# Shared experts in pieces of two products, projections and output in parts, and seven shared blocks behind the routed experts

## The chip, the cores and the metric

One Trainium2 chip, one of its cores. The metric is the time of one execution on the device in microseconds; the median of several executions counts. A profile of one execution comes with it. PE is TensorE, DVE is VectorE, ACT is ScalarE, POOL is GpSimd, SP is SyncE, which only issues DMAs.

## The reference

One transformer layer of fp32 over `x` of shape (4, 1024, 256): `x + attention(xn) + ffn(xn)`, with `xn = layernorm(x)` for both branches.

```python
qkv = (xn @ W_qkv + b_qkv)                       # 16 heads of 16, rotary on q and k
attn = softmax(q @ k.T / sqrt(16))               # 1024 x 1024 per head and batch
attention = (attn @ v) @ W_out + b_out

scores = sigmoid(xn @ w_gate.T)                  # 16 experts, 4 groups of 4
w, idx = grouped_top4(scores)                    # 2 best groups, 4 best experts, weights normed
routed = sum over 4 experts of w * swiglu(xn, w1_e, w3_e, w2_e)     # hidden size 128
shared = silu(xn @ w1_s.T) * (xn @ w3_s.T) @ w2_s.T                 # hidden size 256
ffn = routed + shared
```

## The kernel before

Everything runs in one stream of 256 **steps** of attention, into which all other work is mixed by hand. A group is one batch (b, 0 to 3) and four heads (g, 0 to 3); each of the 16 groups has 16 steps, s = 0 to 15. `Attention.step` makes one step:

- Two **quartets** of matmuls. Each of the four matmuls of a quartet uses 32 rows of TensorE and fills one PSUM bank of 128x512. Two are scores for the exponentials of this group (`ps`, L1225, evacuated by ScalarE as `es`, L1234), two are scores for the row maxima of the next group (`pm`, L1183, reduced by VectorE, L1191). The last 16 steps have no next group, and there all eight matmuls are of the first kind.
- Between the quartets (`between`) the **units** of this step: all other work of TensorE.
- After them the product of the step's exponentials with the values (`av`, L1250), one step late. `av_part(2)` makes it whole behind the second quartet. If the next step has no units (`more` is false), `av_part(0)` makes only the first half there, and the next step makes the second half between its quartets.

TensorE takes its instructions strictly in this order (`k.pe`), and so does SP (`k.sp`). All PSUM tiles come from one pool of eight banks (`k.bank`); the bank of each is fixed when the program is built. One bank holds `av` for eight steps.

`pieces(step)` gathers the units of a step. `Attention.own` gives what the attention needs itself: `max_off` (the maxima into q, steps s = 2 and 10), `normalise` (s = 3 and 11), for the batches 1 to 3 projections and their transposes (`project_unit` every other step for 16 steps, `turn_unit` three steps after each), and per half batch the output projection, `finish`, as a turn and in the next step a product of 8 matmuls and two adds to `acc`. Then come the others:

- **Shared experts.** 16 blocks of 256 rows, of three units each (`shared_block`): two of `first(c)`, one for each half of the hidden size, with gate and up products in one bank (`hidden`: tanh on ScalarE, two operations on VectorE), and `last`, the output product of two times two matmuls in one bank and one add of 128x512 to the rows of x (`xb`, loaded by SP, with the bias added by POOL). The block is stored to `acc` in DRAM in the next step. From step 10 three units come in seven steps, up to 36 units (12 blocks); the other four blocks come after the routed experts, two units in five steps (steps 173 to 200). These units come whether or not the step has other work.
- **Routed experts.** Routing on VectorE and POOL from step 9; from step 33 two rows of slots per step are written by indirect DMA (`put`); from step 98 one pair of tiles per step (`expert_units`), 72 pairs and a last output, with their weights loaded by SP two steps ahead; from step 171 two gathers per step (`get`, POOL) and two sums (`add`, L1011, VectorE), onto rows of `acc` that SP loads first.

`acc` of the half batches is fetched by SP (`fetch_acc`) before `finish` adds to it. `reload` brings the transposed input of batches 2 and 3 back from DRAM (1 MB); the first unit of a batch's first shared block calls for the next batch's (`want`), at steps 38 and 66.

A step without units is called **empty** below.

Of the kernel before, what the change touches and what calls it, by code (L numbers as in the profile page):

```python
# [8 lines left out]
F32 = mybir.dt.float32  # L9
I32 = mybir.dt.int32  # L10
AF = mybir.ActivationFunctionType
# [4 lines left out]
P = 128  # L16
# [26 lines left out]
SHARED = ((10, 36),)  # L43
# [6 lines left out]
def kernel(  # L50
# [166 lines left out]
    n_put = NT * TOPK  # L217
    done = {"shared": 0}
    tiles, ex = None, None

    def pieces(step):

        nonlocal tiles
        now = norm.pieces(step, att.own(step))
        while routing_tensor:
            now.append(routing_tensor.pop(0))
        due = 0
        if SHARED[0][0] <= step:
            due = min(SHARED[0][1], 1 + (step - SHARED[0][0]) * 3 // 7)
        if tiles is not None and not tiles:  # L230
            due = min(len(shared), SHARED[0][1] + (step - TILES_FROM - PAIRS) * 2 // 5)
        while done["shared"] < due:
            now.append(shared[done["shared"]])
            done["shared"] += 1
        if step == TILES_FROM:
            tiles = beside.expert_units(ex.enter_context(ex_pool()))
        if tiles:
            now.append(tiles.pop(0))
            if not tiles:
                done["tiles"] = step  # L240
        return now
# [41 lines left out]
class Kit:  # L283


    def __init__(self, tc, banks):
        self.tc, self.nc, self.banks = tc, tc.nc, banks
        self.last_sp = self.last_exp = None
        self.ranking = self.slots_known = False
        self.summed = 0  # L290
# [490 lines left out]
class Beside:  # L781
# [51 lines left out]
    def shared_block(self, blk):  # L833
        k, nc = self.k, self.nc
        b, at = divmod(blk * SL, T)
        st = {"gu": []}

        def first(c):
            def run():
                if c == 0:  # L840
                    st["x"] = self.ff.tile([P, R, C], F32, name=f"xb_{blk}", tag="y", bufs=3)
                    k.sp(st["x"], k.rows(k.xf, blk * R, R))
                    nc.gpsimd.tensor_tensor(
                        st["x"], st["x"], k.bo_sb.unsqueeze(1).to_broadcast([P, R, C]), ALU.add
                    )
                if at == 0 and c == 0:
                    self.want(b)
                fs = slice(c * P, (c + 1) * P)
                st["gu"].append(
                    self.hidden(  # L850
                        self.xnT[b][:, :, at : at + SL],
                        [(k.w1s_sb[:, :, fs], k.w3s_sb[:, :, fs])], f"s{blk}_{c}",
                    )
                )
            return run

        def last():
            po = k.bank([P, R, C], f"pso_{blk}")
            for r in range(R):
                for c in range(FS // P):  # L860
                    k.pe(
                        nc.tensor.matmul(  # L862
                            po[:, r, :],
                            lhsT=st["gu"][c][:, r * P : (r + 1) * P],
                            rhs=k.w2s_sb[:, c, :],
                            start=(c == 0), stop=(c == FS // P - 1),
                        )
                    )
            nc.vector.scalar_tensor_tensor(st["x"], po, 0.5, st["x"], ALU.mult, ALU.add)
            self.later.append(lambda: k.sp(k.rows(k.acc, blk * R, R), st["x"]))  # L870

        return [first(0), first(1), last]

    def want(self, b):

        for n in range(1, B):
            if n not in self.back and n <= b + 1:
                self.reload(n)
# [105 lines left out]
    def get(self):  # L984
# [5 lines left out]
        if kk == 0:  # L990
            self.yg = self.rows.tile([P, TOPK, C], F32, name=f"yg_{t}", tag="yg", bufs=3)
# [33 lines left out]
class Attention:  # L1025
# [7 lines left out]
    def __init__(self, ctx, k, wqkv_sb, bqk_sb, bv_sb, wout_sb, cos_sb, sin_sb):  # L1033
# [26 lines left out]
        self.av, self.accs, self.stores = {}, {}, []  # L1060
# [4 lines left out]
    def project_unit(self, b, t):  # L1065
        self.product(b, t)
        self.rotate(b, t)

    def product(self, b, t):
        nc, k = self.nc, self.k  # L1070
        if t == 0:
# [10 lines left out]
        n0 = t * P  # L1082
        ps = [k.bank([P, HALF], f"pqk_{b}_{t}"), k.bank([P, C + E], f"pv_{b}_{t}")]

        for half, w in ((0, HALF), (1, C if b else C + E)):
            for c in range(NC_):
                k.pe(
                    nc.tensor.matmul(  # L1088
                        ps[half][:, :w],
                        lhsT=self.xnT[b][:, c, n0 : n0 + P],  # L1090
                        rhs=self.wqkv_sb[:, c, half * HALF : half * HALF + w],
                        start=(c == 0),
                        stop=(c == NC_ - 1),
                    )
                )
# [8 lines left out]
        else:  # L1104
# [5 lines left out]
            qk.rearrange("p h d -> p (h d)"), ps[0], self.bqk_sb, ALU.add  # L1110
        ).ins

        nc.scalar.copy(
            self.vv[b][:, t, : H * VS].rearrange("p (h d) -> p h d", d=VS)[:, :, :DH],
            ps[1][:, :C].rearrange("p (h d) -> p h d", d=DH),
        )
        if b == 0:
            nc.scalar.copy(self.logits[:, t, :], ps[1][:, C:])
        self.qk = qk, rot
# [167 lines left out]
    def fetch_acc(self, b, qh):  # L1287
        k = self.k
        t1 = b * TT + qh * 4 + 4
        assert b + 1 < B or k.summed >= t1  # L1290
# [6 lines left out]
    def finish(self, b, qh):  # L1297
# [15 lines left out]
        def product():  # L1313
            acc = self.accs[b, qh]
            for pr in range(2):
                py = k.bank([P, 2, C], f"py_{b}_{qh}_{pr}")
                for i in range(2):
                    for c in range(NC_):
                        k.pe(
                            nc.tensor.matmul(  # L1320
                                py[:, i, :],
                                lhsT=oc[:, c, 2 * pr + i, :],
                                rhs=self.wout_sb[:, c, :],
                                start=(c == 0),
                                stop=(c == NC_ - 1),
                            )
                        )
                part = acc[:, 2 * pr : 2 * pr + 2, :]
                nc.vector.tensor_tensor(part, part, py, ALU.add)
            to = k.outf if b == B - 1 else k.acc  # L1330
            self.stores.append(lambda: k.sp(k.rows(to, b * TT + qh * 4, 4), acc))

        return turn, product
# [11 lines left out]
    def own(self, at):  # L1345
# [16 lines left out]
        if self.projects(at):  # L1362
            out.append(lambda: self.project_unit(*self.projects(at)))
        if self.projects(at - 3):
            out.append(lambda: self.turn_unit(*self.projects(at - 3)))
        if g == 0 and b > 0 and s == 5:
            self.parts = self.finish(b - 1, 1)
            out.append(self.parts[0])
        last = 13 if b + 1 < B else 14
        if g == NG - 1 and s == last:  # L1370
            self.parts = self.finish(b, 0)
            out.append(self.parts[0])
        if g == 0 and b > 0 and s == 6 or g == NG - 1 and s == last + 1:
            out.append(self.parts[1])
        return out

    def step(self, units, more, bits):
# [48 lines left out]
        if g == NG - 1:  # L1426
            if s == (7 if b + 1 < B else 12):
                self.fetch_acc(b, 0)
            if s == 15 and b + 1 < B:
                self.fetch_acc(b, 1)  # L1430

    def last_steps(self):
# [8 lines left out]
        for turn_or_product in self.finish(b, 1):  # L1441
            turn_or_product()
# [59 lines left out]
```

## Time and profile before

| | |
|---|---|
| median of 3 executions | 1421.13 us (1420.94 to 1421.87) |
| profiled execution | 1426.41 us, its span 1424.7 us |
| granted TensorE clock, mean | 0.995 |
| PE, DVE, ACT, POOL busy | 98%, 65%, 55%, 30% of the span |
| DMA | 199 MB, 140 GB/s |
| matmul records | 9878, two for each fp32 matmul |

The span is the time from the first to the last instruction; the profiled execution's time has 1.7 us more around it. The steps are not marked in the trace; step n begins with the es number 4n of ScalarE, here taken from its timeline:

| steps | what lies beside the attention | us |
|---|---|---|
| 9 to 97 | routing, shared experts, puts, projections of batches 1 and 2 | 443.6 |
| 98 to 170 | routed experts, projections of batches 2 and 3 | 524.3 |
| 171 to 203 | gathers, shared experts | 152.0 |
| 204 to 239 | gathers | 131.9 |
| 240 to 255 and the end | last group, output | 53.1 |

A busy time is the union of an engine's instructions, with the ends of matmuls modelled; a row of the timeline has start and length in us; a row of groups has its count, then its busy time in us and the mean length of one in ns, then idle time before it.

### The profile page before, as it was taken

Reading aid. Unit: us, or ns where it says so; the run is one execution under the profiler, and the core shown is the slowest. Engines: PE = TensorE matmul, PEld = TensorE weight load, DVE = VectorE, ACT = ScalarE, POOL = GpSimd, SP = SyncE. Lnnn points to the kernel's source line nnn. Section 1 sums busy time; section 2 is a strip of 40 time slices with the busy share of each in tenths; the row PEclk is TensorE's granted clock in tenths of the full one; section 3 lists DMA queues with packets and bytes.
Section 4 is the critical chain, followed back from the end, with each engine's and each line's share of the span. In section 5 each row is a group of like instructions: output and inputs, shape, how many; then the busy total and the mean of one; then the engine's idle time right before and its main releaser. Section 6 shows DMA issues by size and latency. Waiting matters only on the chain.

```text
span 1424.7 us, 26637 instructions
## 1 busy us (share of the span) xinstructions
PE 1400.7 (98%) x9878; PEld 683.9 (48%) x9878; DVE 925.4 (65%) x1702; ACT 780.8 (55%) x1586; POOL 423.0 (30%) x498
## 2 busy tenths in 40 slices
PE   7899999999999999999999999999999999999998
PEld 4443344443444344566566665656564344433333
DVE  6878867668766675444555555554445888899941
ACT  4565544455544555555555555554555555566575
POOL 5401503664443445220000000001224444455500
PEclk9899999999999999999999999999999999999999
DMA  5134743523242224446666666665551334333310
GB/s 185 62 124 167 256 169 115 174 75 104 91 139 92 90 78 141 148 149 189 209 209 201 203 197 216 190 208 168 169 152 56 109 119 130 112 108 111 104 39 30
DMA packets 136673, 199.15 MB, mean 140 GB/s; under 512 B 13920, under 2 KB 99040, under 8 KB 136288
## 3 DMA queue, kind: packets, MB, share of 16 engines
q1 hardware_dynamic: 103088, 137.78, 30.7%
q0 software_dynamic: 12288, 33.57, 7.6%
q10 hardware_dynamic: 21168, 26.10, 5.2%
q8 instruction: 78, 1.28, 0.4%
q14 instruction: 51, 0.42, 0.1%
HBM read 124.01 MB, written 79.69 MB: 143 GB/s over the span
## 4 chain that ended last, share of the span: by engine, by line
PE 97%; DVE 1%; ACT 1%; DMA 0%; issue 0%; POOL 0%; ACTq 0%; DVEq 0%
PE pm L1183 22%; PE ps L1225 19%; PE av L1250 19%; PE ph_r L813 9%; PE exy L947 5%; PE ph_s L813 4%; PE pqk L1088 4%; PE ext L938 2%; PE pso L862 2%; PE py L1320 2%; PE ptr L1164 2%; PE pv L1088 2%; PE po L1274 1%; PE pmt L1206 1%; DVE mx L1191 1%; PE pt L472 1%
## 5 line engine op out<-in xcount | busy, mean ns | idle before, releaser
L1234 ACT ACTIVATE es<-ps 128x512 f32<-128x512 f32 x1024 | 554.8, 596 | 412.6 <-PE ps L1225 228.1
L1191 DVE TENSOR_REDUCE mx<-pm 128x1 f32<-128x512 f32 x1024 | 659.5, 683 | 167.0 <-PE pm L1183 103.4
L1183 PE MATMUL pm<-kT,qT 32*128 32x512 f32 x1792 | 523.1, 641 | 1.4 <-ACT kT L1169 1.4
L1225 PE MATMUL ps<-q,kT 32*128 32x512 f32 x1792 | 506.2, 640 | 0.9 <-DVE q L1211 0.8
L1250 PE MATMUL av<-es,vv 128*32 128x512 f32 (+1 forms) x2576 | 287.4, 517 | 0.0
L1225 PEld LDWEIGHTS ps<-q,kT 32*128 32x128 f32 x1792 | 143.3, 183 | 168.0 <-ACT es L1234 85.1
L1183 PEld LDWEIGHTS pm<-kT,qT 32*128 32x128 f32 x1792 | 157.7, 183 | 66.2 <-issue 23.3
L1250 PEld LDWEIGHTS av<-es,vv 128*32 128x32 f32 x2576 | 51.5, 108 | 240.5 <-issue 216.4
L903 POOL DMA_INDIRECT xs<-rows,slot_i x128 | 123.7, 967 | 128.3 <-DVE mx L1191 111.5
L994 POOL DMA_INDIRECT yg<-ys,slot_i x128 | 121.8, 952 | 126.5 <-DVE mx L1191 121.0
L821 DVE SCALAR_TENSOR_TENSOR th_r<-th_r,ph_r 128x256 f32<-128x256 f32 x72 | 30.3, 421 | 195.9 <-ACT th_r L820 195.9
L1128 POOL TENSOR_TENSOR rot<-qk,sin_sb 128x256 f32<-128x256 f32 x56 | 39.5, 726 | 372.5 <-DVE qk L1109 372.0
L813 PE MATMUL ph_r<-xT,w 128*128 128x128 f32 x1152 | 140.5, 275 | 0.5 <-ACT xT L941 0.5
L813 PEld LDWEIGHTS ph_r<-xT,w 128*128 128x128 f32 x1152 | 134.4, 192 | 0.8 <-ACT xT L941 0.7
L1183 PE MATMUL pm<-qkT,qkT 32*128 32x512 f32 x256 | 78.5, 640 | 1.3 <-DVE mx L1191 1.3
L947 PE MATMUL exy<-w,gu_r 128*128 128x256 f32 x288 | 77.3, 391 | 0.0
L1225 PE MATMUL ps<-q,qkT 32*128 32x512 f32 x256 | 75.4, 640 | 0.3 <-DVE gu_s L823 0.3
L820 ACT ACTIVATE th_r<-ph_r 128x256 f32<-128x256 f32 x72 | 27.7, 384 | 81.1 <-PE ph_r L813 81.1
L947 PEld LDWEIGHTS exy<-w,gu_r 128*128 128x128 f32 x288 | 50.0, 190 | 28.7 <-issue 19.7
L1011 DVE SCALAR_TENSOR_TENSOR sum<-yg,wk,sum 128x256 f32<-128x256 f32 x128 | 60.7, 474 | 0.0
L953 ACT ACTIVATE y<-exy 128x512 f32<-128x512 f32 x72 | 43.8, 608 | 17.7 <-PE exy L947 17.4
L1080 POOL MEMSET vv<- 128x128 f32 x4 | 1.3, 318 | 143.6 <-ACT es L1234 143.6
(178 smaller groups left out, 1224.7 us busy)
## 6 DMA issues: line engine op xcount, KB each, us to landing
w<-we SPq DMA_DIRECT2D x144, 384.0 KB
xs<-zero ACTq DMA_DIRECT2D x8, 2304.0 KB
xg<-xs SPq DMA_DIRECT2D x72, 256.0 KB
ys<-y SPq DMA_DIRECT2D x72, 256.0 KB
acc<-acc SPq DMA_DIRECT2D x14, 512.0 KB
xb<-in_x_dram SPq DMA_DIRECT2D x16, 256.0 KB
acc<-xb SPq DMA_DIRECT2D x16, 256.0 KB
we<-in_w_dram ACTq DMA_DIRECT2D x4, 1024.0 KB
```

The source lines that it names most:

```text
L813: nc.tensor.matmul(ph[:, n, at], lhsT=w[n][:, c, :], rhs=xT[:, c, at], start=(c == 0), stop=(c == NC_ - 1),)
L903: put = nc.gpsimd.indirect_dma_start(out=k.xs, out_offset=bass.IndirectOffsetOnAxis(ap=k.slot_i[:, t, kk : kk + 1], axis=0), in_=self.rows ...
L947: nc.tensor.matmul(py[:, r, :], lhsT=gus[i][:, r * P : (r + 1) * P], rhs=got[i][1][:, r, 2 * NC_ * F :], start=True, stop=True,)
L953: nc.scalar.activation(y, py, AF.Copy, scale=0.5)
L994: get = nc.gpsimd.indirect_dma_start(out=self.yg[:, kk, :], out_offset=None, in_=k.ys, in_offset=bass.IndirectOffsetOnAxis(ap=k.slot_i[:, ...
L1011: nc.vector.scalar_tensor_tensor(sm[:, 0, :], yg[:, kk, :], k.wk[:, t, kk : kk + 1], sm[:, 0, :], ALU.mult, ALU.add)
L1088: nc.tensor.matmul(ps[half][:, :w], lhsT=self.xnT[b][:, c, n0 : n0 + P], rhs=self.wqkv_sb[:, c, half * HALF : half * HALF + w], start=(c = ...
L1183: nc.tensor.matmul(ps, lhsT=self.qT[b, g // 2][rows, g % 2, qt * P : (qt + 1) * P], rhs=self.kT[b, g // 2][rows, g % 2, hf * HALF : (hf + ...
L1191: k.pace = nc.vector.tensor_reduce(out=self.mx_of[b, g, qt // 4][hf][:, qt % 4, j, :], in_=ps, axis=AX.X, op=ALU.max,).ins
L1225: nc.tensor.matmul(ps, lhsT=self.kT[b, g // 2][rows, g % 2, kc * P : (kc + 1) * P], rhs=self.q2[b, g, qh][rows, :], start=True, stop=True,)
L1234: k.last_exp = nc.scalar.activation(e, ps, AF.Exp, scale=DH**-0.5).ins
L1250: nc.tensor.matmul(av[32 * j : 32 * j + 32, cols], lhsT=self.vv[b][:, kc, h * VS : h * VS + 32], rhs=es[j][:, cols], start=(kc == 0), stop ...
```

## The change

Shared blocks are cut finer: `gate(c)` and `up(c)` are one product each (4 matmul records of 128x256, a bank of their own), `last(r)` is the output product of 128 rows with an add of 128x256: six **half pieces** a block, 96 in all. Nine blocks (54 pieces) come before step 98, seven (42 pieces) after the routed experts. A piece is given to a step that has no units; to one that has, only when the count is behind a line. `project_unit` becomes the product for q and k with the rotation, and in the next step that for the values; the product of `finish` is four products, one in each of four steps, with an add of 128x256 each. The transposed input of batch 3 is reloaded at step 110, `fetch_acc` of a second half batch comes at s = 3 of the next group instead of s = 15. `shared_rows` only serves the assertions that `acc` is stored before it is read.

```diff
-SHARED = ((10, 36),)
+SHARED_FROM = 10
+SHARED_FIRST = 9
+RELOAD_AT = 110
...
+    k.at_step[RELOAD_AT] = lambda: beside.reload(B - 1)
...
-        due = 0
-        if SHARED[0][0] <= step:
-            due = min(SHARED[0][1], 1 + (step - SHARED[0][0]) * 3 // 7)
-        if tiles is not None and not tiles:
-            due = min(len(shared), SHARED[0][1] + (step - TILES_FROM - PAIRS) * 2 // 5)
-        while done["shared"] < due:
-            now.append(shared[done["shared"]])
+        n, first = done["shared"], SHARED_FIRST * len(shared) // (NT * P // SL)
+        if tiles is None and SHARED_FROM <= step < TILES_FROM and n < first:
+            left = TILES_FROM - 1 - step
+            late = n < first - left * (first + 6) // (TILES_FROM - SHARED_FROM)
+        elif tiles is not None and not tiles and n < len(shared):
+            m, since = n - first, step - TILES_FROM - PAIRS
+            late = m < since * 4 // 5 if since <= 25 else m < 18 + (since - 25) * 24 // 34 - 4
+        else:
+            late = None
+        if late or late is not None and not now:
+            now.append(shared[n])
             done["shared"] += 1
...
+        def half(c, n):
+            ph = k.bank([P, SL], f"ph_s{blk}_{c}_{n}")
+            w = (k.w1s_sb, k.w3s_sb)[n]
+            for i in range(NC_):
+                k.pe(
+                    nc.tensor.matmul(
+                        ph, lhsT=w[:, i, c * P : (c + 1) * P],
+                        rhs=self.xnT[b][:, i, at : at + SL],
+                        start=(i == 0), stop=(i == NC_ - 1),
+                    )
+                )
+            return ph
...
-        def first(c):
+        def gate(c):
...
+                ph = half(c, 0)
+                th = st["th"] = self.ff.tile([P, SL], F32, name=f"th_s{blk}_{c}", tag="th")
+                nc.scalar.activation(th, ph, AF.Tanh, scale=0.5)
+                nc.vector.scalar_tensor_tensor(th, th, 1.0, ph, ALU.add, ALU.mult)
             return run
+        def up(c):
+            def run():
+                ph = half(c, 1)
+                gu = self.ff.tile([P, SL], F32, name=f"gu_s{blk}_{c}", tag="gu", bufs=3)
+                nc.vector.tensor_tensor(gu, st["th"], ph, ALU.mult)
+                st["gu"].append(gu)
+            return run
...
+        def last(r):
+            def run():
+                po = k.bank([P, C], f"pso_{blk}_{r}")
...
+                x = st["x"][:, r, :]
+                nc.vector.scalar_tensor_tensor(x, po, 0.5, x, ALU.mult, ALU.add)
+                if r == R - 1:
+                    self.later.append(store)
+            return run
...
-        return [first(0), first(1), last]
+        return [gate(0), up(0), gate(1), up(1)] + [last(r) for r in range(R)]
...
-            if n not in self.back and n <= b + 1:
+            if n not in self.back and n <= min(b + 1, B - 2):
...
-        def product():
-            acc = self.accs[b, qh]
-            for pr in range(2):
-                py = k.bank([P, 2, C], f"py_{b}_{qh}_{pr}")
...
+        def product(i):
+            py = k.bank([P, C], f"py_{b}_{qh}_{i}")
...
+            nc.vector.tensor_tensor(acc[:, i, :], acc[:, i, :], py, ALU.add)
...
+        return [turn] + [lambda i=i: product(i) for i in range(4)]
...
         if self.projects(at):
-            out.append(lambda: self.project_unit(*self.projects(at)))
+            b1, t1 = self.projects(at)
+            out.append(lambda: self.product(b1, t1, (0,)))
+            out.append(lambda: self.rotate(b1, t1))
+        if self.projects(at - 1):
+            out.append(lambda: self.product(*self.projects(at - 1), (1,)))
...
-        if g == 0 and b > 0 and s == 6 or g == NG - 1 and s == last + 1:
-            out.append(self.parts[1])
+        if self.parts:
+            out.append(self.parts.pop(0))
...
-        if g == NG - 1:
-            if s == (7 if b + 1 < B else 12):
-                self.fetch_acc(b, 0)
-            if s == 15 and b + 1 < B:
-                self.fetch_acc(b, 1)
+        if g == NG - 1 and s == (7 if b + 1 < B else 12):
+            self.fetch_acc(b, 0)
+        if g == 0 and b > 0 and s == 3:
+            self.fetch_acc(b - 1, 1)
```

## The prediction

> **What bounds the kernel now.** Read in this order: busy table, windows by stage, groups by form, then TensorE's timeline.
>
> The page, its busy table:
>
> ```profile
> span 1424.7 us, 26637 instructions
> ...
> PE 1400.7 (98%) x9878; PEld 683.9 (48%) x9878; DVE 925.4 (65%) x1702; ACT 780.8 (55%) x1586; POOL 423.0 (30%) x498
> ```
>
> TensorE is busy throughout, so it looks as if only its work counts, and the change removes none. The window over the late steps says the same of a stretch almost without extra work, with VectorE near it:
>
> ```profile
> core 0: us, PE busy (x) PEld busy (x) DVE busy (x) ACT busy (x) POOL busy (x), PEclk, DMA share, GB/s
> 1243.00:1361.00 118.00, 118.00 (x1000) 40.77 (x992) 110.90 (x209) 71.53 (x133) 57.66 (x61) 1.00 0.37 105
> ```
>
> A busy row hides two losses, which TensorE's timeline of a step *without other work* shows (start, length, count):
>
> ```profile
> 1342.94 0.69 PE L1183 MATMUL pm<-kT,qT 32*128 32x512 f32 x1
> ...
> 1344.01 0.64 PE L1250 MATMUL av<-es,vv 128*32 128x256 f32 x8
> 1344.58 0.69 PE L1225 MATMUL ps<-q,kT 32*128 32x512 f32 x1
> 1344.59 0.69 PE L1183 MATMUL pm<-kT,qT 32*128 32x512 f32 x1
> 1344.59 0.69 PE L1225 MATMUL ps<-q,kT 32*128 32x512 f32 x1
> 1344.85 0.69 PE L1183 MATMUL pm<-kT,qT 32*128 32x512 f32 x1
> ...
> 1345.90 0.64 PE L1250 MATMUL av<-es,vv 128*32 128x256 f32 x8
> ```
>
> Four row-tiled matmuls go side by side (a quartet, two passes, 1.07 us). Here the fourth starts 0.26 us after its mates, and all behind it shift by as much; a busy row does not show it. It waits for a PSUM bank. The first readers of the quartet of 1342.94, from the timeline of all engines:
>
> ```profile
> 1344.10 0.69 DVE L1191 TENSOR_REDUCE mx<-pm 128x1 f32<-128x512 f32 x1 [0.16 <-PE ps L1225]
> 1344.20 0.60 ACT L1234 ACTIVATE es<-ps 128x512 f32<-128x512 f32 x1 [0.90 <-PE ps L1225]
> ```
>
> The reduction ends at 1344.79, and the matmul starts at 1344.85: **a bank comes back 1.91 us after the start of the quartet that filled it**. The exponential ends as early, 1344.80. Of 8 banks av holds one and the last quartet four; three are free, and the next quartet, 1.64 us later, needs a fourth: 1.91 - 1.64 = 0.27. Second, the av product is cut in halves here, 2 x 0.57 (1344.01 to 1344.58) in place of one of 0.99.
>
> The same lengths where a piece of shared work lies between the quartets:
>
> ```profile
> 1150.44 1.99 PE L862 MATMUL pso<-w2s_sb,gu_s 128*128 128x256 f32 x8
> 1152.37 0.69 PE L1183 MATMUL pm<-kT,qT 32*128 32x512 f32 x1
> ...
> 1153.44 1.06 PE L1250 MATMUL av<-es,vv 128*32 128x512 f32 x8
> 1154.43 0.69 PE L1225 MATMUL ps<-q,kT 32*128 32x512 f32 x1
> ```
>
> No start is late. The piece takes 1.93: 8 x 0.216 (spacing of its records) and 0.20 for going into the full array and back. Av whole: 0.99. The nearest rows to a half piece are these transposes, 0.87 us of work as well, but in two banks:
>
> ```profile
> 1103.38 1.09 PE L1164 MATMUL ptr<-ident,pad 128*128 128x128 f32 x8
> ...
> 1104.41 0.69 PE L1183 MATMUL pm<-kT,qT 32*128 32x512 f32 x1
> 1104.60 0.69 PE L1225 MATMUL ps<-q,kT 32*128 32x512 f32 x1
> ```
>
> Here the fourth is 0.19 late. Last, groups by form:
>
> ```profile
> L1250 PE MATMUL av<-es,vv 128*32 128x512 f32 x1520 | 203.3, 604 | 0.0
> ...
> L1250 PE MATMUL av<-es,vv 128*32 128x256 f32 x1056 | 84.3, 391 | 0.0
> ...
> L823 DVE TENSOR_TENSOR gu_s<-th_s,ph_s 128x256 f32<-128x256 f32 x32 | 13.4, 420 | 1.1
> ...
> L869 DVE SCALAR_TENSOR_TENSOR xb<-pso,xb 128x512 f32<-128x512 f32 x16 | 11.1, 691 | 11.1 <-PE pso L862 6.3 <-issue 4.8
> ```
>
> A halved step has 16 half records: 1056 / 16 = 66 steps are cut.
>
> **So a step is a sum.** 2 x 1.07 + 0.99 + (0.20 + own work), or, when empty, 2 x 1.07 + 1.14 + wait. Held against the distances of the first es of each step (ScalarE's timeline), this fits steps 30 to 239 to 0.05 where no wait is due (4.63 and 5.06 with a shared unit, 6.42 with a pair), and what empty steps are over it is their wait (3.52 against 3.28 in steps 205 to 208). The exceptions: steps 10 to 19 (VectorE sorts the routing; its durations add up to 48.7 us in 47.9), 22 to 25 (routing's matmuls), 67 to 69 and 75 to 77, some 5 us late in all, where no cause is seen. The profiled execution took 1426.41 (span 1424.7 and 1.7 around it), 5.3 over the median 1421.13. I take the change as a difference and apply it to both.
>
> **The change part by part.** I lay both schedules out by their formulas. Empty steps from 9 to 239: before 64 (26 up to step 97, 10 in 171 to 203, 28 in 204 to 239); after 7, since all up to 230 that do not have maxima, transposes or projections get a half piece or a part. **57 are filled.**
>
> *Filling a step.* Work is only moved, so overhead alone counts: it loses the wait and the cut (1.14 - 0.99 = 0.14, rounded down from the spacings) and pays the change of array (0.20). The wait over the 57, five disturbed ones left out, is 0.14 to 0.49, mean 0.30 (28 at 0.25; those behind a shared unit mostly 0.39). So 0.30 + 0.14 - 0.20 = 0.24 each, 57 x 0.24 = **-13.7**.
>
> *A wait in filled steps.* 80 steps will hold one piece of 4 matmuls, 0.86, alone (71 shared, 9 output or value parts). The trace has no such step. By the bank account, quartet to quartet is 1.07 + 0.20 + 0.86 = 2.13, the piece takes one bank, two are free, two come back at 1.91: slack 0.22, wait 0. Then 1.07 + 0.99 = 2.06 to the next: slack 0.15, as in today's steps with shared work, which show none. The same account gives 0.21 for a max_off step (1.70 apart, measured 0.22), and a wait for the transposes, whose second bank makes a third release necessary. Bounds: 0 (shared steps) to 0.19 (transposes), and no gain below 0, since the parts of the step are fixed. That is 0 to 15; nearest are the shared steps, with the same bank and readers; 0.03 for banks badly dealt: **+2.4**.
>
> *Steps 10 to 19.* VectorE sets the pace; its work there falls by one operation of 0.42, so filling gains little: **+1.1** against the above (0 to 2).
>
> *Steps with max_off or normalise alone* grow from 26 to 30 (+0.22 each), transposes alone fall from 10 to 3 (-0.14 each): **-0.1**.
>
> *Projections and output in parts.* pqk 1.72 in one step, pv 0.86 in the next; four products of 0.86 for one of 3.46. In steps with pairs this is even (9.88 + 3 x 6.42 against 4 x 7.29). At the very end the last add is 0.42, not 0.69: **-0.3**.
>
> *VectorE.* 16 adds of pso and 16 of py turn into 64 of half the width: 32 x (2 x 0.42 - 0.69) = 4.8 us more busy. Hidden: late steps need 4 reductions at 0.61 spacing, two sums at 0.47 and a piece at 0.42, 3.8 of 4.2. If that cover goes, see the second rival.
>
> *Moved DMAs and queues.* Three blocks go behind the experts, each with an xb load and an acc store on SP, an add of 1.27 on POOL (between gathers that take 1.9 of 4.2 there) and two tanh. Nothing on the path waits: a block's load has four pieces' time. Tightest is the last: acc of block 15 is stored in step 231, and SP then holds the load of row 30's sum in that step until it lands. SP's longest wait on an acc load was 2.5; the add comes 1.5 steps, 5 us, later. Cost 0, else 2.5 once. The reload of 1 MB at step 110 goes among weight loads at a DMA share of 0.58 (181 GB/s, so some 310 when full, my estimate): 3.4, hidden by weights fetched two steps (12.8) ahead; else 3.4. Fetching acc four steps later leaves three steps to its use.
>
> Sum: -13.7 + 2.4 + 1.1 - 0.1 - 0.3 = **-10.6**: 1421.1 - 10.6 = **1410.5** (a profiled execution some 1416). By stage: steps 9 to 97, 443.6 to 423; 98 to 170, 524.3 to 525; 171 to 203, 152.0 to 147; 204 to 239, 131.9 to 145.5.
>
> **Rivals.**
>
> *Slower: the bank wait moves into the filled steps.* Banks are dealt at build time. If the second quartet gets the bank of the second reduction, which starts 0.61 after the first and is back at 1.91 + 0.61 = 2.52, it waits 2.52 - 2.13 = 0.39 in each of those steps. For it: empty steps behind a shared unit wait 0.39, not 0.25, so badly dealt banks exist; a gate piece holds its bank through tanh and one VectorE operation. Against: none in 28 steps with a whole shared unit. 80 x 0.39 = 31 in place of 2.4: -10.6 + 28.8 = +18, 1439; it decides from 0.16 a step (13.0 / 80), and slower by 0.2% from 0.20, 1424. Chance 0.10.
>
> *VectorE becomes the bound in the late steps.* A cycle of 8 needs 6 x 3.8 + 4.1 (max_off) + 4.0 (normalise) = 30.9 of 6 x 4.2 + 2 x 4.0 = 33.2: it holds on average. If all 4.8 us of extra work showed, 1415. Chance 0.06. [...]
>
> *No difference: half pieces wait as the transposes do,* 0.14 to 0.19: 80 x 0.16 = 13 eats the gain: 1419 to 1423. Chance 0.10.
>
> *It does not do what it says:* a late load (block 15's sum, the reload) stalls VectorE or TensorE, 2.5 and 3.4: 1416. Chance 0.04.
>
> **How the numbers follow.** Forecast 0.70: 1405 (no wait in filled steps, late stretches gone) to 1416. A measurement of this kernel tells about 0.2%, 2.8 us, from no change. Faster (below 1418.3): 0.70 + 0.06 + 0.04 = 0.80; same 0.10; slower 0.10. The range takes in most of the third rival and leaves out the first: 1404 to 1421.
>
> **What would show it.** Half-width av records: 66 cut steps fall to about 10 (two or three at the start, seven after step 230), 1056 to some 160. Steps with one piece last 4.20, quartets in them unsplit; 4.4 or more is the first rival, 4.35 the third. Steps 205 to 230 mostly 4.20 with VectorE idle before its reductions; if it never idles, the second. The forecast is wrong if matmul starts inside quartets are late by 0.16 or more in filled steps, or if the stage from 98 to 170 grows.

## The result, and the profile after

The changed kernel takes **1415.37 us** (median of 5, 1414.26 to 1417.86) beside 1421.87 for the kernel before in the same comparison: a ratio of **0.9958, 95% interval 0.9947 to 0.9969**, 6.5 us less by the medians where 10.6 were forecast. The profiled execution took 1417.86 (span 1416.2), the slowest of the five.

The page after, its busy table:

```profile
span 1416.2 us, 25822 instructions
...
PE 1390.9 (98%) x9438; PEld 656.3 (46%) x9438; DVE 929.1 (66%) x1734; ACT 783.6 (55%) x1586; POOL 424.1 (30%) x498
```

VectorE has 3.7 us more, where 4.8 were costed, and TensorE is as full as before: again the row does not show what changed. TensorE's timeline of a late step does (start, length, count):

```profile
1224.98 0.69 PE L1277 MATMUL ps<-q,kT 32*128 32x512 f32 x1
...
1226.05 1.13 PE L892 MATMUL pso<-w2s_sb,gu_s 128*128 128x256 f32 x4
1227.11 0.69 PE L1235 MATMUL pm<-kT,qT 32*128 32x512 f32 x1
1227.12 0.69 PE L1277 MATMUL ps<-q,kT 32*128 32x512 f32 x1
1227.13 0.69 PE L1235 MATMUL pm<-kT,qT 32*128 32x512 f32 x1
1227.13 0.69 PE L1277 MATMUL ps<-q,kT 32*128 32x512 f32 x1
...
1228.18 1.06 PE L1302 MATMUL av<-es,vv 128*32 128x512 f32 x8
1229.18 0.69 PE L1277 MATMUL ps<-q,kT 32*128 32x512 f32 x1
```

A half piece lies between the quartets, the four matmuls of the second start within 0.02 us of each other, av is whole, and from one step's first quartet to the next's it is 4.20 (1224.98 to 1229.18), the sum with no wait. Groups by form:

```profile
L1302 PE MATMUL av<-es,vv 128*32 128x512 f32 x1960 | 263.6, 608 | 0.0
...
L1302 PE MATMUL av<-es,vv 128*32 128x256 f32 x176 | 14.1, 391 | 0.0
```

176 half records are 11 cut steps; 160 were forecast. The stages, from the distances of ScalarE's es (us, one profile each; the later profile of the changed kernel and the last column, the version with both adds moved, are of the fourth comparison below):

| steps | before | forecast | changed | changed, later profile | best |
|---|---|---|---|---|---|
| 9 to 19 | 53.4 | | 60.6 | 57.2 | 52.1 |
| 20 to 97 | 390.3 | | 364.9 | 365.7 | 364.8 |
| 9 to 97 | 443.6 | 423 | 425.5 | 422.9 | 416.9 |
| 98 to 170 | 524.3 | 525 | 525.6 | 525.6 | 526.9 |
| 171 to 203 | 152.0 | 147 | 146.8 | 146.5 | 146.3 |
| 204 to 239 | 131.9 | 145.5 | 145.8 | 146.1 | 144.8 |

The column of before is of an execution 5.3 us above its median, and its excess lies in steps 20 to 97: the last experiment's version of that kernel, which runs at the usual time, has 384.1 there instead of 390.3. So some 6 of the 18 to 21 us by which steps 9 to 97 fall in this table belong to that execution and not to the change.

One stage went against the forecast: steps 9 to 19, 7.2 us longer instead of some 1. It lies in step 15 (7.72 us, 5.22 before) and step 19 (10.59, 4.72 before). POOL's and VectorE's timelines in step 19 (in brackets idle time and what ended it):

```profile
164.87 0.51 POOL L633 TENSOR_TENSOR rk<-rk,ge_e 128x160 f32<-128x160 f32 x1
171.24 1.26 POOL L868 TENSOR_TENSOR xb<-xb,bo_sb 128x512 f32<-128x512 f32 x1 [5.86 <-DMA xb<-in_x_dram]
172.46 0.45 POOL L632 TENSOR_TENSOR rk<-rk,ge_e 128x128 f32<-128x128 f32 x1
```

```profile
169.82 0.69 DVE L1243 TENSOR_REDUCE mx<-pm 128x1 f32<-128x512 f32 x1 [0.65 <-PE pm L1235]
173.36 0.38 DVE L631 TENSOR_TENSOR ge_e<-msk 128x64 f32<-128x64 f32 x1 [2.84 <-POOL rk L633]
173.66 0.68 DVE L1243 TENSOR_REDUCE mx<-pm 128x1 f32<-128x512 f32 x1
```

POOL's bias add of the second shared block stands in front of the routing's last rank operations and waits 5.86 us for its rows; VectorE's next compare needs a buffer that these rank operations free; the reduction behind it, which frees a PSUM bank, comes at 173.66 instead of some 170.5; and TensorE runs dry. Then the clock goes. Windows over the same time:

```profile
core 0: us, PE busy (x) PEld busy (x) DVE busy (x) ACT busy (x) POOL busy (x), PEclk, DMA share, GB/s
...
170.00:174.00 4.00, 1.69 (x10) 0.69 (x7) 1.16 (x3) 1.46 (x3) 2.76 (x6) 0.97 1.06 401
174.00:178.00 4.00, 3.61 (x10) 0.70 (x10) 2.24 (x6) 0.60 (x1) 1.85 (x6) 0.50 0.79 307
178.00:182.00 4.00, 4.00 (x20) 1.66 (x20) 1.29 (x2) 1.47 (x3) 0.00 (x0) 0.67 0.00 0
```

TensorE idles 2.7 us, then works at half its clock for 6.8 us (0.50, part of the next window): a stall of 3 us turns into 6.

### The profile page after: what moved, and what is told of

It reads as the page before. It is cut to its first block, busy times and chain, and to the rows that moved or that the text cites. A ratio compares the mean times of both kernels' runs of the same rounds, so it can differ in the third digit from the quotient of the medians.

```text
span 1416.2 us, 25822 instructions
## 1 busy us (share of the span) xinstructions
PE 1390.9 (98%) x9438; PEld 656.3 (46%) x9438; DVE 929.1 (66%) x1734; ACT 783.6 (55%) x1586; POOL 424.1 (30%) x498
## 4 chain that ended last, share of the span: by engine, by line
PE 96%; DVE 2%; DMA 1%; ACT 1%; issue 0%; POOL 0%; ACTq 0%; POOLq 0%; DVEq 0%
PE ps L1277 20%; PE pm L1235 20%; PE av L1302 18%; PE ph_r L823 9%; PE exy L982 5%; PE ph_s L855 4%; PE pqk L1149 4%; PE py L1371 2%; PE pso L892 2%; PE pv L1149 2%; PE ext L973 2%; PE ptr L1216 2%; PE pmt L1258 1%; PE po L1326 1%; DVE mx L1243 1%; PE pt L482 1%
## 5 line engine op out<-in xcount | busy, mean ns | idle before, releaser
L1235 PE MATMUL pm<-kT,qT 32*128 32x512 f32 x1792 | 511.7, 643 | 1.4 <-ACT kT L1221 1.4
L1302 PE MATMUL av<-es,vv 128*32 128x512 f32 (+1 forms) x2136 | 277.4, 590 | 0.0
L1235 PEld LDWEIGHTS pm<-kT,qT 32*128 32x128 f32 x1792 | 147.6, 183 | 64.7 <-DVE mx L1243 26.8
L1302 PEld LDWEIGHTS av<-es,vv 128*32 128x32 f32 x2136 | 42.9, 108 | 199.6 <-issue 177.7
L1235 PE MATMUL pm<-qkT,qkT 32*128 32x512 f32 x256 | 73.4, 640 | 0.0
L1047 DVE SCALAR_TENSOR_TENSOR sum<-yg,wk,sum 128x256 f32<-128x256 f32 x128 | 63.7, 498 | 0.3 <-DMA yg<-ys,slot_i 0.3
```

What stands on the lines that cost most here:

```text
L1047: nc.vector.scalar_tensor_tensor(sm[:, 0, :], yg[:, kk, :], k.wk[:, t, kk : kk + 1], sm[:, 0, :], ALU.mult, ALU.add)
L1235: nc.tensor.matmul(ps, lhsT=self.qT[b, g // 2][rows, g % 2, qt * P : (qt + 1) * P], rhs=self.kT[b, g // 2][rows, g % 2, hf * HALF : (hf + ...
L1302: nc.tensor.matmul(av[32 * j : 32 * j + 32, cols], lhsT=self.vv[b][:, kc, h * VS : h * VS + 32], rhs=es[j][:, cols], start=(kc == 0), stop ...
```

## The experiments

There are four comparisons, each on one chip with its own runs of the kernel before, which took 1421.87, 1426.7, 1428.36 and 1421.26 (so ratios are compared across them). The first is that of the result.

**The changed kernel again**, in the second comparison and in the fourth.

> The changed kernel once more, beside the others of this batch. Theory: steps 9 to 19 take 60 to 61 us again (53.4 before), with TensorE's clock at half for one or two stretches of 3.41 us in steps 15 to 20, since their causes (the place of the bias add on POOL, VectorE's order) are fixed by the program; the time is some 1415. Rival: the lowered clock is an accident of the one profiled execution as the one at 426 us in the kernel before was; then steps 9 to 19 take some 54 to 56, and the time is still 1415, because the other executions had no such stretch.

> The changed kernel, on the chip of the kernels of this batch, for the comparison: 0.9958 to 0.9965 of the kernel before.

1421.91, ratio 0.9965 (0.9951 to 0.9979), and 1416.88, ratio 0.9968 (0.9957 to 0.998): 4.8 and 4.4 us of gain, less than in the first comparison. Step 19 took 10.31 and 9.91, each time with a half-clock stretch of 6.83 us behind it; so the stall of step 19 is no accident. Step 15 took 6.06 and 5.06, without such a stretch, so that part of the first profile did not come back, and the stage from 9 to 19 took 58.8 and 57.2, not 60 to 61. In the second comparison steps 171 to 239 took 297.6, 5 more than in the others: steps 187, 209 and 226 at 6.08, 5.35 and 5.12.

**First piece at step 20.**

> The changed kernel with its first shared piece at step 20 instead of 10, so nothing of a shared block lies among the routing's operations of VectorE and POOL. The same 54 pieces are done by step 97. Theory (the pieces and the bias add among the ranking cause the 7.2 us that steps 9 to 19 gained): steps 9 to 19 come back to 53 to 54 us, no stretch of lowered clock there, steps 20 to 97 as in the changed kernel (365 us, plus at most 1), and the time is 5 to 7 us below the changed kernel, some 1409. Rival (the stalls come from the ranking and its loads, and the pieces only lie beside them): steps 9 to 19 stay at 58 to 61 and the time is that of the changed kernel within 2 us.

```diff
-SHARED_FROM = 10
+SHARED_FROM = 20
```

Median 1425.75 against 1421.91: *slower* by 4, ratio 0.9991 (0.9982 to 1.0). The profiled execution was the fastest of eleven, 1422.01, as fast as that of the changed kernel, so the profile shows where time moved but not the 4 us. In it steps 9 to 19 came down to 51.3, as the theory has it (though a half-clock stretch of 3.41 us at 153.2 stayed), but 20 to 97 rose from 364.9 to 374.8 where 1 was allowed. Six more pieces lie there, 53 for 47, at 0.86 each 5.2; the rest is lateness, most of it in steps 60, 61 and 68. So the stall does come from what was moved, and the cure was wrong: in steps 10 to 19 these pieces cost little (the version with both adds moved has them there and takes 52.1), in later steps their full length.

**POOL's add of the block three pieces later.**

> The changed kernel with POOL's bias add of a shared block moved from the block's first piece (gate of the first half) to its fourth (up of the second half); its load by SP stays where it is. Theory (step 19 is late because POOL, in order, waits 5.9 us in the add of block 1 for a load that queues behind the zero fill, and the routing's POOL operations and through them VectorE wait behind it): step 19 falls from 10.6 us to 4 to 5, and the second, 6.8 us long stretch of half clock goes; step 15 stays at 7 to 8 us, since its stall has another cause (VectorE in order). In all 4 to 6 us below the changed kernel, some 1410. Rival (step 19 is late because VectorE has too much to do in these steps): step 19 stays above 8 us and the time within 2 us of the changed kernel.

```diff
-                    nc.gpsimd.tensor_tensor(st["x"], st["x"], ...)
...
+                if c == 1:
+                    with self.tc.issue_after(k.last_exp):
+                        nc.gpsimd.tensor_tensor(st["x"], st["x"], ...)
```

1421.05, 0.9965 (0.9952 to 0.9979); step 19 still 9.75. This refutes nothing: in POOL's order the add kept its place in front of the last eight rank operations and waited 5.54 us there. The order on POOL was fixed when the program was built, and the place in the source did not decide it. The edit did not make the change that it was to test; the kernel after the next does.

**The av product never cut, in the kernel before.**

> The kernel before with one thing changed: from step 9 on the product with the values is never cut in halves (always whole behind the second quartet), so an empty step has its two quartets 1.07 apart and nothing between them. Nothing else moves. Bank theory (a bank comes back 1.91 us after the start of the quartet that filled it; three are free): the second quartet of an empty step needs a fourth bank at 1.07 and waits 0.84; the step takes 2 x 1.07 + 0.99 + 0.84 = 3.97 instead of 3.52, and over the 57 to 64 empty steps the kernel gets 25 to 29 us slower, some 1448. Rival (empty steps lose by the cut itself, not by banks): each of these steps gets 0.14 shorter, some 8 us faster, 1413.

```diff
-        att.step(now, bool(then) and (...), bits)
+        att.step(now, step >= 9 or bool(then) and (...), bits)
```

1432.55, ratio 1.0038 (1.0025 to 1.0051): 5.9 us slower, not 25, and not faster as the rival had it. TensorE's timeline of an empty step:

```profile
1251.81 0.69 PE L1225 MATMUL ps<-q,kT 32*128 32x512 f32 x1
...
1252.37 1.00 PE L1183 MATMUL pm<-kT,qT 32*128 32x512 f32 x2
...
1252.78 0.59 PE L1225 MATMUL ps<-q,kT 32*128 32x512 f32 x1
1252.79 1.00 PE L1183 MATMUL pm<-kT,qT 32*128 32x512 f32 x2
```

The four matmuls of a quartet no longer start together, and the step takes 3.85 instead of 3.52: 3.13 of work and 0.72 of wait, where the bank account gives 0.84. So the direction is right: without the half av product between its quartets an empty step pays more for banks than it saves. The size is wrong over the whole kernel. Where empty steps follow each other each takes 0.33 more, not 0.45, but the step behind them gives 1.03 back (step 209: 3.95 becomes 2.92), so the 28 of steps 204 to 239 cost 5.6 in all; beside a longer step the distances between the es shift from one to the next and the sum of the two hardly changes (4.63 and 4.10 become 5.06 and 3.85).

**The add behind the ranking.**

> The changed kernel with one order set by hand: POOL's bias add of the second shared block is queued behind the last of the routing's rank operations on POOL (in the changed kernel it stands in front of the last eight of them, and waits there 5.9 us for its load). Pieces, loads and everything else stay. Theory (that wait holds up POOL, through it VectorE's compares and the reductions behind them, and through these TensorE): step 19 falls from 10.3 to 10.6 us to below 5.5, the long stretch of half clock at 174 us goes, steps 15 and 16 stay as they are; 5 to 6 us below the changed kernel. Rival (VectorE has too much to do there whoever waits): step 19 stays above 8, time within 2 us.

```diff
+            k.ranked = eng.tensor_tensor(...)
...
+                    with self.tc.issue_after(k.ranked) if blk == 1 else ExitStack():
                         nc.gpsimd.tensor_tensor(st["x"], st["x"], ...)
```

1417.62, ratio **0.9928** (0.9915 to 0.9942), against 0.9965 and 0.9968 of the changed kernel on other chips: some 5 us. Step 19 takes 4.73, the stage 53.2; the late steps are not touched (171 to 239 take 298.7). POOL's timeline, then windows:

```profile
172.13 0.27 POOL L632 TENSOR_TENSOR rk<-rk,ge_e 128x32 f32<-128x32 f32 x1 [1.34 <-DVE ge_e L631]
172.35 0.27 POOL L633 TENSOR_TENSOR rk<-rk,ge_e 128x32 f32<-128x32 f32 x1
172.57 1.27 POOL L871 TENSOR_TENSOR xb<-xb,bo_sb 128x512 f32<-128x512 f32 x1
```

```profile
170.00:174.00 4.00, 4.00 (x25) 1.21 (x22) 2.60 (x8) 1.55 (x4) 2.47 (x6) 1.00 1.06 406
174.00:178.00 4.00, 4.00 (x28) 1.27 (x28) 2.95 (x5) 2.45 (x5) 0.60 (x2) 1.00 0.85 330
```

The add now waits for nothing, TensorE is never idle in these windows, and the clock stays at 1.00, with the DMA as busy as before (1.06). This shows the cause of step 19: the order on POOL.

**No add for the seven late blocks.** In the changed kernel VectorE's and POOL's timelines of step 207 read:

```profile
1233.68 1.40 DVE L1047 SCALAR_TENSOR_TENSOR sum<-yg,wk,sum 128x256 f32<-128x256 f32 x1
```

```profile
1233.53 1.27 POOL L868 TENSOR_TENSOR xb<-xb,bo_sb 128x512 f32<-128x512 f32 x1 [3.35 <-issue]
```

The sum, 0.48 long elsewhere, ends 0.3 after POOL's add. The reductions behind it are late, and with them a bank:

```profile
1235.52 0.69 PE L1235 MATMUL pm<-kT,qT 32*128 32x512 f32 x1
1235.82 0.69 PE L1277 MATMUL ps<-q,kT 32*128 32x512 f32 x1
```

> The changed kernel without POOL's bias add for the seven shared blocks behind the routed experts (so those rows lack the output bias; nothing else is left out). Theory (VectorE's two-input operations stand still while POOL's add of 1.27 us runs: sums of 0.48 us took 1.31 to 1.53 in steps 179, 207 and 223, a 0.19 one took 1.25 in step 215): these four operations have their usual length, the steps 180, 208, 216 and 224 last 4.20 instead of 4.40 to 4.63, and the stage from 171 to 239 is 1.3 us shorter by the first profile of the changed kernel, up to 4 by the second, in which steps 187, 209 and 226 were late as well. Rival (the late loads and gathers are what these steps wait for): these steps stay within 0.1 and the time within 1 us.

```diff
+                    if blk < SHARED_FIRST:
                         nc.gpsimd.tensor_tensor(st["x"], st["x"], ...)
```

1415.79, ratio **0.9917** (0.9903 to 0.993). Steps 180, 208, 216 and 224 all last 4.20, and 171 to 239 take 291.6: 1.0 below the first and the third profile of the changed kernel, 6.0 below the second, and 7.1 below the version with the add behind the ranking, on the same chip. Steps 187, 195, 209, 217 and 226, late there or in the kernel with only the add of the second block moved, are all as computed. The version with both adds moved (below), which has none in these steps either, takes 291.2 and 291.1. So POOL's adds set off that lateness too, strongly in the profiles of the second and third comparison and hardly in those of the first and fourth; what makes the difference is not known. How an add of 1.27 leads to steps late by up to 2 us one or two steps later is not seen.

**Projections and output whole.**

> The changed kernel with projections and output products whole in one step again; the half pieces of the shared experts and their places by the same rule stay. The steps that values and output parts filled are free for pieces, and the rule gives them some. Theory of the prediction (parts are worth nothing of their own, 9.88 + 3 x 6.42 against 4 x 7.29 us; only that no step stays empty counts): within 2 us of the changed kernel, the stage from 98 to 170 at 524 to 526. Rival (a long unit costs more than its parts, since exponentials and reductions run dry beside it, or parts lengthen other steps): more than 2 us off, to one side or the other, and seen in the stage from 98 to 170.

```diff
-            out.append(lambda: self.product(b1, t1, (0,)))
+            out.append(lambda: self.product(b1, t1))
...
-            out.append(lambda: self.product(*self.projects(at - 1), (1,)))
...
-        return [turn] + [lambda i=i: product(i) for i in range(4)]
+        return [turn, lambda: [product(i) for i in range(4)]]
```

1427.53, ratio 0.9992 (0.9983 to 1.0001): some 4 us above the changed kernel, as the rival has it, but not where it looked: 98 to 170 took 525.0, so parts beside the experts are worth nothing, as forecast. Steps 171 to 203 took 155.5 instead of 146.5 to 149.7, with 182, 188, 196 and 198 at 5.59, 5.46, 5.69 and 6.79. Late adds of POOL are in this stage as well, so how much the parts save there stays open.

**Both adds moved ("best").** The second block's add stands behind the ranking; the bias of the last seven blocks is added beside the routed experts and stored to `acc`, from where the late block loads.

> Both of the above, with the whole result: the bias add of the second block behind the ranking, and the bias of the last seven blocks added in steps 118 to 157, beside the routed experts: rows of x loaded by SP, added by POOL, stored to acc three steps later, and loaded from acc when the late block starts. If both theories hold: step 19 below 5.5, steps 180, 208, 216 and 224 at 4.20, and 6 to 9 us below the changed kernel, less what the seven adds cost beside the experts (at most one VectorE operation held up by 1.3 us each, with 2.4 us of idle time before it there, so 0 to 2 us, I take 0). If both fall: within 2 us of the changed kernel, or slower by the loads and stores.

> The version with both bias adds moved, beside the changed kernel on one chip: 10 to 13 us below it.

```diff
+    for n in range(SHARED_FIRST, NT * P // SL):
+        k.at_step[BIAS_AT + 6 * (n - SHARED_FIRST)] = lambda n=n: beside.bias_ahead(n)
...
-                    k.sp(st["x"], k.rows(k.xf, blk * R, R))
+                    k.sp(st["x"], k.rows(k.acc if blk >= SHARED_FIRST else k.xf, blk * R, R))
```

1410.23, ratio **0.9879** (0.9863 to 0.9894), and in the fourth comparison 1409.76, **0.992** (0.9908 to 0.9933), 7.1 us below the changed kernel on that chip, where 10 to 13 were expected. Steps 9 to 19 take 52.1, and the adds cost 1.3 beside the experts (526.9). On the chip of the third comparison it is 7.4 us below the version with only the second block's add moved (1417.62), which prices the seven late adds there; steps 171 to 239 fall from 298.7 to 291.2. This version is the fastest, and varies little: 1409.8 and 1410.2 on chips where the kernel before took 1421.3 and 1428.4.

**Pieces two at a time**, to price the empty steps alone.

> The version with both bias adds moved, but the 96 half pieces given two at a time, by lines of 3 pairs in 10 steps before step 98 and 21 pairs in 58 steps from step 170: the same work in the same stages, with 54 empty steps instead of 7. Theory of the prediction (an empty step costs 0.24 us more than its work, as it waits 0.30 for a bank and cuts the av product): 47 x 0.24 = 11 us above the version with one piece a step, empty steps at 3.5 to 3.9, 376 more half-width... that is 16 half av records for each cut step, some 700 to 800 in all. Rival (the gain of the change came from what went behind the experts and from the POOL adds, not from filled steps): within 3 us of the version with one piece a step.

```diff
-        if late or late is not None and not now:
-            now.append(shared[n])
+        while done["shared"] < due:
+            now.append(shared[done["shared"]])
```

1423.09, ratio 1.002 (1.0011 to 1.0028), **13.3 us** above the version with one piece a step on the same chip; by the two profiles (spans 1420.3 and 1409.0) 11.3. 11 were expected, 0.24 for each of 47 steps. Groups by form:

```profile
L1314 PE MATMUL av<-es,vv 128*32 128x256 f32 x896 | 71.6, 391 | 0.0
```

896 are 56 cut steps, 45 more than the 11 of the version with one piece a step (176 records). The empty steps from 171 on last 3.52 to 3.95. The rival, within 3 us, is out: filled steps are what saves. Their price is less sharp. The 13.3 would be 0.30 for each of the 45. But the profiles put 1.8 in step 98, where no step was emptied (10.64 us beside 8.86, TensorE idle 2.33 us for a load of the experts), and 2.0 in steps 9 to 19, where four steps were. Steps 20 to 97 are 4.1 longer and 171 to 239 4.3, with the other 41: 0.20 each.

**The kernel before without its POOL adds.**

> The kernel before without POOL's bias add for the shared blocks from the fourth on (rows that then lack the output bias; nothing else is left out). In its profile the adds of steps 66 and 74 are followed by steps 67 to 69 and 75 to 77 that are some 5 us late in all. Theory (the add sets off the lateness, as in the late steps of the changed kernel): steps 68 and 69 fall from 5.46 and 8.38 to 4.0 and 4.5, 75 to 77 by 1.5 in all, the clock stays at 1.00 at 426 us, and the time is 3 to 7 us below the kernel before. Rival (the 1 MB reload in step 65, or chance): the same steps are late again in its profile, or the kernel before is not late there in most of its runs, and the time is within 1 us.

```diff
+                    if blk < 3:
                         nc.gpsimd.tensor_tensor(st["x"], st["x"], ...)
```

In its profile step 68 is 3.88 instead of 5.46, the clock stays at 1.00 and the span is 1419.7; but step 69 still takes 5.89, and the time is 1421.38 against 1421.26, ratio 1.0001 (0.9992 to 1.001). So the rival holds on this chip: the kernel before runs here as fast with the adds as without, and the lateness in steps 67 to 77 belongs to the execution that was profiled, 5.3 above its median. It is not shown for the chips of the second and third comparison, where the kernel before took 1426.7 and 1428.36 in the median; whether it is late in these steps there was not tried.

## Why the prediction was right, and where it was not

- **What bounds the kernel** (a step as a sum, a bank back 1.91 us after its quartet): held. Steps with one piece last 4.20 in the late stage except where a POOL add was near, and emptied steps cost time again. Its size was off where quartets come 1.07 apart: 0.72 of wait, not 0.84.
- **Filling a step**, -13.7 for 57 at 0.24: right in kind, and shown by the pairs of pieces. Stage by stage these give 0.20 each, so -11.4; by the medians, other lateness included, 0.30.
- **A wait in filled steps**, +2.4: too careful, it is 0. By the stages the two terms together are -11.4 where -11.3 was forecast; that their errors cancel is luck. The first rival (badly dealt banks, 0.39 a step) and the third (0.16) did not come: the second quartets start unsplit.
- **Steps 10 to 19**, +1.1 with bounds of 0 and 2: this step failed. The stage grew by 3.8 to 7.2 in three profiles, step 19 alone by 5.2 to 5.9. The term counted VectorE's operations and not POOL's order: the second block's load came two steps later than before and took longer (issued at 163.65, 7.6 us to the add; before, issued at 153.42, 4.1), and POOL waited 5.86 us for it with the rank operations behind. In the kernel before the same add stood seven rank steps in and waited 1.31. The premise was read too strongly as well: the 48.7 us of VectorE's durations overlap, and its busy time there is 43.43 of 48.00 (the third busy time of this row), so it was not full:

```profile
125.00:173.00 48.00, 47.41 (x312) 18.58 (x312) 43.43 (x87) 23.91 (x45) 22.42 (x31) 1.00 0.71 260
```

- **Moved DMAs and queues**, "cost 0, else 2.5 once": also failed, by less. The loads were in time, as argued; the add of 1.27 itself was not free, for it holds up VectorE (three sums of 0.48 took 1.31 to 1.53 beside it). The seven late adds cost 1.0 us by two profiles of the changed kernel, 6.0 by one, and 7.4 by the medians of the third comparison.
- **Reload, later acc, projections in parts beside the experts**: 98 to 170 at 525.6 for 525. Right.
- **The stages.** 171 to 203 and 204 to 239 came out within 0.5 and 0.6 of the forecast in the two profiles of the table. That 9 to 97 came near it too (425.5 and 422.9 for 423) is luck: the forecast was taken off a profile with some 6 us of its own lateness there, and the stall of step 19 took their place. The stage forecasts also add up to 11.3 less, not 10.6.
- **VectorE the bound in late steps**: it did not come; the late window has 95.22 of 104.00 busy:

```profile
1222.00:1326.00 104.00, 104.00 (x696) 37.37 (x700) 95.22 (x181) 58.24 (x109) 50.66 (x53) 1.00 0.37 110
```

On the chip of the fourth comparison both adds cost 7.1 by the medians (the changed kernel less the version with both moved). The two profiles hold 5.1 of it in steps 9 to 19, 1.5 in 171 to 239 and 0.9 in 20 to 97, and 98 to 170 give back 1.3; the last 0.9 is not located. With both adds moved the change is worth 11.5, near the forecast of 10.6. The forecast is right because its main term is; what was lost, some 7 us there, are the places of two kinds of POOL add in that engine's order: one was behind a term that counted only VectorE, the other was put at nothing.

## What to carry to other kernels

When work is dealt out more finely, list for each engine what the moved unit issues there, and look at what stands behind it *in that engine's queue*: one add of 1.27 us on the least busy engine (30%) cost some 5 of 11.5 us. In steps 10 to 19 the extra TensorE work cost little (steps 9 to 19 took 52.1 us with it and both adds moved, 51.3 without it) and in later steps its full length (0.86 a piece), so the stall there was better cured by order than by moving the work out. And test a place in a queue by reading the order that was built: a moved line of source need not move the instruction.

## What the runs showed of the hardware

**VectorE and POOL hold each other up.** Operations of VectorE with two inputs in SBUF that met a POOL add of 1.27 grew from 0.48 to between 1.31 and 1.53 (three sums of the first profile) and from 0.19 to 1.25, and end within 0.3 of the add; a compare of the ranking took 1.35 beside POOL's rank operation, but 0.52 in the version with both adds moved, where it started at the same time and POOL's operation grew instead, from 1.00 to 1.38. First the first profile, then that version:

```profile
147.81 1.00 POOL L633 TENSOR_TENSOR rk<-rk,ge_e 128x384 f32<-128x384 f32 x1
147.83 1.35 DVE L631 TENSOR_TENSOR ge_e<-msk 128x352 f32<-128x352 f32 x1
149.11 1.27 DVE L1243 TENSOR_REDUCE mx<-pm 128x1 f32<-128x512 f32 x2
```

```profile
148.73 1.38 POOL L636 TENSOR_TENSOR rk<-rk,ge_e 128x384 f32<-128x384 f32 x1
148.74 0.52 DVE L634 TENSOR_TENSOR ge_e<-msk 128x352 f32<-128x352 f32 x1
```

The recorded starts lie 0.01 to 0.02 us apart and do not tell which of the two waits, but step 15 goes with it: in the profiles of the changed kernel, of the versions with an add moved or left out, and of the one with projections whole, it takes 6.06 us or more in the four in which the compare takes 1.35, with 0.60 us of idle TensorE, and 5.06 to 5.08 in the five in which it takes 0.52.

The reductions, with one input and that in PSUM, keep their 0.64 each beside POOL's operation of 149.33 (0.87 long). The other way round, four adds that began within 0.2 us after a sum took 1.44 to 1.55 (first and third profile of the changed kernel). In the profile the wait is inside the length, not in the idle time: compare lengths within a group. Why the two hold each other up is not shown.

**Short idle times of TensorE were followed by half its clock in some places, and not in others.** In step 15 of the first profile TensorE was idle for 0.60 us at 151.6, and from 153.3 its clock was at half for 3.41 us. The idle times of step 19 in the three profiles of the changed kernel, 2.43 to 2.70 us, were each followed by 6.83 us of half clock; in the profile of before 1.31 us at 423.2 was followed by 3.41. But the length of the idle time does not settle it. With the add behind the ranking TensorE was idle for the same 0.60 us at 152.5, and the clock stayed at 1.00; so it did after 1.21 us at 124.4 in the first profile, and in the version with pieces two at a time after 2.33 us at 546.5. Windows of the add behind the ranking, then of pieces two at a time:

```profile
149.00:157.00 8.00, 7.40 (x43) 2.96 (x40) 7.17 (x12) 3.27 (x7) 5.63 (x7) 1.00 0.80 295
```

```profile
545.00:550.00 5.00, 2.67 (x24) 2.43 (x23) 0.69 (x2) 2.57 (x7) 0.00 (x0) 1.00 0.92 319
550.00:555.00 5.00, 5.00 (x41) 2.52 (x40) 2.60 (x5) 2.15 (x6) 0.00 (x0) 1.00 0.87 278
```

What decides is not shown.
